# Batch 0 of a fused attention and FFN block: q turned elsewhere, weights in another order, and both ends of the kernel rearranged

## The chip, the core and the metric

The kernel runs on one core of a Trainium2 chip. The time is device microseconds of one execution, from launch to the last result; lower is better. Everything is float32.

The core's engines work in parallel, each through its own queue of instructions in order, and wait for each other by semaphores: TensorE (PE) for matmuls, VectorE (DVE), ScalarE (ACT), GpSimd (POOL), and SyncE (SP), which here only issues DMAs. ACT issues a few DMAs too.

## The reference

```python
x = L0_attn_x                                   # 8 x 1024 x 256
xn = layernorm(x)                               # no scale, no shift
q, k, v = split(xn @ qkv_w + qkv_b)             # 16 heads of 16
q, k = q / |q|, k / |k|                         # per head
kv  = einsum('bhnd,bhne->bhde', k, v)           # no softmax: 16 x 16 per head
att = einsum('bhnd,bhde->bhne', q, kv) @ proj_w + proj_b
ffn = relu(xn @ W1 + b1) @ W2 + b2              # 256 -> 1024 -> 256
out = x + att + ffn
```

## The kernel before

The kernel loops over the 8 batches. A batch is 1024 rows, 8 tiles of 128 rows (NT = 8, a half is HT = 4 tiles). The order of the work is written by hand: `tc.manual_schedule()` keeps each engine's instructions in the order in which the Python code issues them.

**Matmuls by sums.** Most products are done as 2 x 2 blocks with seven products instead of eight. That needs sums and differences of blocks of both operands: of W1 (`sums_of_w1`), W2 (`sums_of_w2`), the q,k weights (`sums_of_wqk`), the turned x (`sums_of_x`, `s3_of_x`), the hidden layer (`sums_of_h`), the turned q (`sums_of_q`) and k with x (`g_sums`). Nearly all of them run on POOL, through `sums_of_b` (L184-189) and `sums_of_a` (L191-197), four instructions each.

**A batch in steps.**
1. *Norm.* `norm_stats` (L254, L257, root on ACT L259), `norm_scale` (reciprocal L266, and `nmr` = -mean/std, L269), `norm_apply` on ACT (L278) or DVE (L282). For batch b+2 this is done during batch b.
2. *Turn of x.* `turn_x` transposes squares of 32 x 32 on DVE (L304) and lets 16 DMAs of SP (L306) bring each to its partitions. Batch 0 has no time for that: its tiles are transposed on PE and copied by ACT (`turn_tile`, L923, L924).
3. *`hidden(b)`*: twelve steps of `first`, `fifth` and `last` make the relu layer (L660 on PE, L672 on DVE, L667 on ACT). Between the steps, a table (`first_steps` for batch 0, `later_steps` otherwise) puts the small work: k^T x (`mix_g`), kv (`mix_kv`), kv @ proj_w (`mix_m`), scaling q by its norm (L488), turning q.
4. *`project_by_sums(b+1)`*: q and k of the next batch (L420 on PE, adds L426 on DVE, then on POOL the rest of the bias, L464, and k's scaling, L488). Batch 0 has its own `project` (L337, L343), which runs in the first 25 us and goes tile by tile.
5. *`second(b)`*: hidden @ W2 and q @ M in one accumulation (L785). In its middle, `mix_g_by_sums(b+1)` (L590) multiplies the sums that POOL has made of k and x (L557). Results are joined (L826), turned back on DVE (L817), added to x on POOL (L822) and stored by SP (L831).

**q in batch 0.** In every later batch q is turned by `turn_q`: four transposes on DVE and 16 DMAs of SP. Batch 0 uses `turn_on_pe` (L286-296): 16 transposes on PE (L292) into four banks of PSUM and four copies on ACT, between `hidden(0)` and `project_by_sums(1)`.

**The end.** In batch 7 the second half of the rows is turned back on PE (L838) and stored by ACT (L889) in three pieces, tiles 0 and 1, tile 2, tile 3. The first half goes the usual way: L817 on DVE, L822 on POOL, four stores of SP (L831).

**Buffers.** All bank-sized results share seven banks of PSUM. `turn_x`, `turn_q` and `g_sums` share one buffer ("turn"); q and k of all batches share one ("qk").

Of the kernel before, what the change touches and what calls it, by code (L numbers as in the profile page):

```python
# [9 lines left out]
F32 = mybir.dt.float32  # L10
AF = mybir.ActivationFunctionType
ALU = mybir.AluOpType
# [4 lines left out]
def kernel(  # L17
# [35 lines left out]
    P = 128  # L53
# [94 lines left out]

    def load_rest():

        load_halves(projw_sb, proj_w)
        load_halves(w2_sb, w2)
        for i, v in enumerate((proj_b, b2)):
            for j in range(R):
                nc.sync.dma_start(
                    out=ob[ts(j, S), i, :],
                    in_=v.rearrange("(j m c) -> j c m", m=2, c=S)[j],
                )
# [50 lines left out]
    def sums_of_w2():  # L209
        sums_of_b(  # L210
            nc.gpsimd, [w2_sb[:, ts(k, FH), ts(m, HC)] for k in range(2) for m in range(2)],
            [w2t[:, i, :, :] for i in range(3)],
        )
        nc.gpsimd.tensor_tensor(ob[:, 2, :], ob[:, 0, :], ob[:, 1, :], ALU.add)

    def halves(tt):
# [66 lines left out]
                    xn, xt, mv[:, i, 0:1], rstd[:, i : i + 1], ALU.subtract, ALU.mult  # L283
                )

    def turn_on_pe(dst, src, name, halves=(0, 1), copies=(nc.scalar.copy, nc.scalar.copy)):  # L286

        for h in halves:
            for kc in range(KC):
                tp = bank([P, HT, P], f"tp{name}_{h}_{kc}")  # L290
                for i in range(HT):
                    nc.tensor.transpose(tp[:, i, :], src[:, h * HT + i, ts(kc, P)], ident)  # L292
                copies[kc](
                    dst[:, kc, ts(h, HP), :, :].rearrange("p u m w -> p u w m"),
                    tp.rearrange("p (u w) m -> p u w m", w=2),
                )

    def turn(dst, src, name):


# [19 lines left out]
    def project(b, within={}, behind={}, held_to=0):  # L320

        xnT = xnTs[b]
        if b not in qks:
            qks[b] = one.tile([P, NT, 2 * C], F32, tag="qk", name=f"qk_{b}")
        qk = qks[b]
        late, held = [], []
        for h in range(2):
            ss = small.tile([P, HT, 2 * H], F32, tag="ssk" if h else "ssq", name=f"ss_{b}_{h}", bufs=1)  # L330
            for s in range(2):
                norms_of[b, h, s] = ss[:, :, ts(s, H)]
            for i in range(HT):
                t = h * HT + i
                pq = bank([P, 512], f"pq_{b}_{t}")
                for kc in range(KC):
                    nc.tensor.matmul(  # L337
                        pq, xnT[:, kc, t // 2, :, t % 2], wqkv_sb[:, kc, 0 : 2 * C],
                        start=(kc == 0), stop=(kc == KC - 1), skip_group_check=True,
                    )  # L340
                    if kc == 0:
                        within.get(t, lambda: None)()
                nc.vector.tensor_tensor(qk[:, t, :], pq, qkvb_sb[:, 0 : 2 * C], ALU.add)  # L343

                def square(t=t, ss=ss, i=i):
                    sq = work.tile([P, 2 * C], F32, tag="yt", name=f"sq_{b}_{t}")
                    nc.scalar.activation(sq, qk[:, t, :], AF.Square)
                    return lambda: nc.vector.tensor_reduce(
                        ss[:, i, :], sq.rearrange("p (g d) -> p g d", d=D), AX.X, ALU.add
                    )  # L350

                held.append(square)
                while held and t >= held_to:
                    late.append(held.pop(0)())
                    while len(late) > 1:
                        late.pop(0)()
                behind.get(t, lambda: None)()
        while late:
            late.pop(0)()
# [41 lines left out]
            sq.rearrange("p w (g d) -> p w g d", d=D), AX.X, ALU.add,  # L401
        )

    def project_by_sums(b):


        xnT, xS = xnTs[b], xSs[b]
        qks[b] = one.tile([P, NT, 2 * C], F32, tag="qk", name=f"qk_{b}")
        ss = small.tile([P, NT, H], F32, tag="ssk", name=f"ssk_{b}", bufs=1)
        a11, a12, s3, a22 = halves(xnT)  # L410
        s1, s2, s4 = xS
# [25 lines left out]
        for g in range(2):  # L437
            a, c_, d, e = (banks[g][s] for s in "acde")
            mm(a, a11, b11, g, True, False)
            u1 = add(tmp("u1", g), a, bk)  # L440
            mm(e, s1, t1, g, True, False)
            mm(c_, s2, t2, g, True, True)
            u2 = add(tmp("u2", g), c_, u1)
            u2s.append(u2)
            mm(d, s3, t3, g, True, False)
            u3 = add(tmp("u3", g), d, u2)
            add(part_of_qk(b, 1, g, 1), e, u3)
            while late:
                late.pop(0)()
            late.append(squares_of(b, 1, g, 1, ss))  # L450
# [34 lines left out]
    def scale(eng, b, h, s):  # L485
# [3 lines left out]
            part, part,  # L489
            norms_of[b, h, s].unsqueeze(3).to_broadcast([P, HT, H, D]), ALU.mult,  # L490
        )

    def scale_q(b, h):
        scale(nc.vector, b, h, 0)

    def turn_q(b):

# [242 lines left out]
    def first_steps(b):  # L740

        lo, hi, fold = range(HT), range(HT, NT), fold_bias_of_v()
        of_k, of_q = norms_of_first(1), norms_of_first(0)
        return {
            0: [lambda: load_squares(b), lambda: norm_apply(b + 1, lo)],
            1: [lambda: next(of_k)] * 3 + [lambda h=h: scale(nc.gpsimd, b, h, 1) for h in range(2)],
            2: [lambda: shift(b)],
            4: [
                lambda: norm_stats(b + 1, hi), lambda: norm_scale(b + 1, hi, True),
                lambda: norm_apply(b + 1, hi), lambda: next(of_q), lambda: next(of_q),  # L750
                lambda: next(of_q), lambda: mix_g(b), lambda: next(fold),
            ] + [lambda: turn_x(b + 1)] * R,
            5: [sums_of_w2, lambda: next(fold), lambda: next(fold)],
            6: [lambda: shift(b + 1), lambda: scale_q(b, 0)],
            7: [lambda: mix_kv(b)],
            8: [lambda: g_sums(b + 1, 0), lambda: scale_q(b, 1)],
            10: [lambda: mix_m(b)],
            11: [lambda: load(b + 2)],
        }

    def later_steps(b):
        return {
            0: [lambda: g_sums(b + 1, 0)] if b + 1 < B else [],
            1: [lambda: mix_kv(b)],
            2: [lambda: scale_q(b, 0)],
            3: [lambda: scale_q(b, 1)],
            4: [lambda: mix_m(b)],
            5: [lambda: turn_q(b)],
            6: [lambda: turn_q(b)],
            7: [lambda: turn_q(b)],  # L770
            8: [lambda: turn_q(b)],

            11: [lambda: sums_of_q(b)],
        }
# [15 lines left out]
    def second(b, early=lambda: None, between=lambda: None):  # L790
# [21 lines left out]
        def turn_back(n, m, y):  # L812

            yt = tmp("yt").rearrange("p a b c -> p (a b c)").rearrange(
                "p (u w r c) -> p u w r c", w=2, r=R, c=S
            )
            nc.vector.transpose(  # L817
                yt.rearrange("p u w r c -> p u r w c"),
                y.rearrange("p u (s r) w -> p u r w s", r=R),
            )  # L820
            xh = xq[:, n, :, :, ts(m, S)].rearrange("p r t c -> p t r c")
            nc.gpsimd.tensor_tensor(xh, xh, yt.rearrange("p u w r c -> p (u w) r c"), ALU.add)  # L822

        def join(n, m, bank_, u):
            y = tmp("y")
# [2 lines left out]

        def store(n):
            for j in range(R):  # L830
                nc.sync.dma_start(out=squares_v(out, b, n, j), in_=xq[ts(j, S), n])  # L831

        def back_on_pe(m, y, tiles, name):

# [94 lines left out]


    norm_stats(0, (0,))
    scale_and_apply(0)
    turn_tile(0)
    keep_warm(3)
    norm_stats(0, (1,))
    norm_stats(0, (2,))
    scale_and_apply(1)
    norm_stats(0, (3,))
    scale_and_apply(2)
    scale_and_apply(3)  # L940
# [3 lines left out]
    def tiles_2_3():  # L944
        for t in (2, 3):
            turn_tile(t)
        norm_stats(0, (4, 5))
        norm_stats(0, (6, 7))
        norm_scale(0, (4, 5), True)
        norm_scale(0, (6, 7), True)  # L950
        norm_apply(0, (4, 5))
        norm_apply(0, (6, 7))

    def tiles_4_to_7():
        for t in range(HT, NT):
# [13 lines left out]
        3,  # L969
    )  # L970
    norm_scale(1, range(HT), True)
    s3_of_x(0)
    sums_of_wqk()
    load_rest()
    for b in range(B):
        if b > 0:
            load_squares(b, (0,) if b == B - 1 else (0, 1))
# [3 lines left out]
                load(B, (HT, NT))  # L981
        hidden(b)
        if b == 0:
            qTs[0] = one.tile([P, KC, NP, P, 2], F32, tag="qT", name="qT_0")
            turn_on_pe(qTs[0], qks[0], "q_0")
            sums_of_q(0)
        if b + 1 < B:
            project_by_sums(b + 1)
            g_sums(b + 1, 1)

            def early():
                if b + 2 < B:
                    norm_stats(b + 2, range(NT))
                    norm_scale(b + 2, range(NT), True)

            def between():
                g_sums(b + 1, 2)
                norms_of_q(b + 1)

            out_parts = second(b, early, between)  # L1000
        else:
            out_parts = second(b)
# [41 lines left out]
```

## Time and profile before

| | us |
|---|---|
| median of 3 runs | 616.42 (616.12 to 616.46) |
| the profiled execution | 616.35 |
| its span, first to last instruction | 614.6 |
| PE busy in the span | 607.1 |
| DVE, POOL, ACT busy | 417.1, 421.4, 212.6 |
| PE's first matmul of the projection | 5.91 |
| last row of PE ends | 609.4 |
| last instruction of DVE ends | 609.7 |

The profile's times count from the first instruction of the span; some 1.8 us of the execution lie outside of it. In a row of a timeline the columns are start, duration, engine, line, operation, output and inputs, shape, and how many instructions were merged; a bracket names idle time of that engine before the row, and what ended it. A float32 matmul shows as two passes: 0.43 for 512 columns; a transpose of 128 x 128 takes 0.11.

### The profile page before, as it was taken

The numbers are of one execution on the slowest core, as the hardware profiler recorded it, in microseconds if no ns is written. First come the engines' busy times: TensorE is split into PE (matmuls) and PEld (weight loads), VectorE is DVE, ScalarE is ACT, GpSimd is POOL, SyncE is SP. The second block draws the span as 40 slices with busy tenths as digits, with TensorE's granted clock in tenths as the row PEclk, the third lists the DMA queues.
The fourth block names the chain that finished last, engine by engine and source line by source line (L and its number), as shares of the span: only waits on it lengthen the run. The fifth ranks groups of instructions, "written<-read, shape, count | busy, mean of one in ns | idle before, by whom it ended". The sixth has DMA issues, their size and how long they took to land.

```text
span 614.6 us, 6728 instructions
## 1 busy us (share of the span) xinstructions
PE 607.1 (99%) x2055; PEld 350.8 (57%) x2055; DVE 417.1 (68%) x746; ACT 212.6 (35%) x369; POOL 421.4 (69%) x345
## 2 busy tenths in 40 slices
PE   8999999999999999999999999999999999999996
PEld 5466765466644756447464484644755456644454
DVE  7886774876758776587665876577864777537823
ACT  4656223351324414243251532425223352103400
POOL 3699992699727995479944899349992499914701
PEclk9999999999999999999999999999999999999999
DMA  8633002760038400482005900158002550005302
GB/s 276 120 70 110 0 0 61 149 135 0 1 81 188 74 1 1 110 189 45 0 13 125 184 22 1 28 124 170 22 0 48 127 102 0 0 11 128 70 0 68
DMA packets 139940, 43.84 MB, mean 71 GB/s; under 512 B 135928, under 2 KB 136832, under 8 KB 139904
## 3 DMA queue, kind: packets, MB, share of 16 engines
q1 hardware_dynamic: 139184, 42.37, 31.1%
q10 hardware_dynamic: 720, 1.05, 0.5%
q8 instruction: 16, 0.26, 0.2%
q14 instruction: 20, 0.16, 0.1%
HBM read 20.32 MB, written 8.39 MB: 47 GB/s over the span
## 4 chain that ended last, share of the span: by engine, by line
PE 97%; DVE 1%; DMA 1%; ACT 0%; SPq 0%; issue 0%
PE poa L785 11%; PE poe L785 11%; PE pod L785 10%; PE pha L660 9%; PE phd L660 9%; PE phe L660 9%; PE poc L785 6%; PE phc L660 4%; PE pqa L420 4%; PE pqe L420 4%; PE pqd L420 4%; PE gpd L590 2%; PE gpe L590 2%; PE gpa L590 2%; PE pqc L420 2%; PE pq L337 1%
## 5 line engine op out<-in xcount | busy, mean ns | idle before, releaser
L822 POOL TENSOR_TENSOR xq<-xq,yt_o 128x512 f32<-128x512 f32 x30 | 38.0, 1265 | 127.3 <-DVE yt_o L817 127.3
L667 ACT ACTIVATE hT<-hT,b_sb 128x512 f32<-128x512 f32 x96 | 68.7, 721 | 61.4 <-DVE hT L672 56.7
L193 POOL TENSOR_TENSOR hS<-hT 128x512 f32<-128x512 f32 x31 | 47.0, 1517 | 34.3 <-ACT hT L667 34.3
L660 PE MATMUL pha<-xnT,w_sb 128*128 128x512 f32 x128 | 65.4, 592 | 0.0
L398 ACT ACTIVATE sq<-qk 128x512 f32<-128x512 f32 x56 | 33.8, 627 | 82.0 <-DVE qk L426 68.6
L785 PE MATMUL poa<-hT,w_sb 128*128 128x512 f32 x128 | 57.6, 592 | 0.0
L672 DVE TENSOR_TENSOR hT<-phe,u 128x512 f32<-128x512 f32 x64 | 43.7, 685 | 6.9 <-PE phe L660 5.3
L195 POOL TENSOR_TENSOR hS<-hT,hS 128x512 f32<-128x512 f32 x31 | 39.6, 1277 | 2.4
L817 DVE STREAM_TRANSPOSE yt_o<-y_o 128x512 f32<-128x512 f32 x30 | 33.3, 1109 | 11.7 <-ACT y_o L875 9.3
L194 POOL TENSOR_TENSOR hS<-hS,hT 128x512 f32<-128x512 f32 x31 | 39.5, 1273 | 2.4
L197 POOL TENSOR_TENSOR hT<-hT 128x512 f32<-128x512 f32 x31 | 41.0, 1322 | 0.0
L686 ACT COPY u<-pha 128x512 f32<-128x512 f32 x32 | 18.4, 575 | 56.8 <-PE pha L660 56.8
L785 PEld LDWEIGHTS poa<-hT,w_sb 128*128 128x128 f32 x128 | 23.8, 190 | 24.2 <-issue 23.9
L660 PEld LDWEIGHTS pha<-xnT,w_sb 128*128 128x128 f32 x128 | 23.7, 190 | 22.9 <-issue 22.2
L672 DVE TENSOR_TENSOR u<-phc,u 128x512 f32<-128x512 f32 x32 | 21.8, 680 | 19.6 <-ACT u L686 10.0
L667 ACT ACTIVATE hT<-pha,b_sb 128x512 f32<-128x512 f32 x32 | 21.8, 683 | 35.6 <-PE pha L660 35.6
L660 PE MATMUL phc<-xS,w1t 128*128 128x512 f32 x64 | 32.7, 592 | 0.0
L660 PE MATMUL phd<-xnT,w1t 128*128 128x512 f32 x64 | 32.7, 592 | 0.0
L660 PE MATMUL phe<-xS,w_sb 128*128 128x512 f32 x64 | 32.7, 592 | 0.0
L660 PE MATMUL phd<-xnT,w_sb 128*128 128x512 f32 x64 | 32.7, 592 | 0.0
L660 PE MATMUL phe<-xS,w1t 128*128 128x512 f32 x64 | 32.7, 592 | 0.0
L278 ACT ACTIVATE x<-x,nmr,rstd 128x256 f32<-128x256 f32 x60 | 30.6, 589 | 2.6 <-DVE nmr L269 2.6
(203 smaller groups left out, 1322.4 us busy)
## 6 DMA issues: line engine op xcount, KB each, us to landing
x<-in_L_attn_x_dram SPq DMA_DIRECT2D x15, 512.0 KB, 5.6
xq<-in_L_attn_x_dram SPq DMA_DIRECT2D x60, 128.0 KB, 3.5
out_dram<-xq SPq DMA_DIRECT2D x60, 128.0 KB, 2.9
xnT<-turn_x SPq DMA_DIRECT2D x112, 64.0 KB, 2.1
qT<-turn_q SPq DMA_DIRECT2D x112, 64.0 KB, 2.3
w_sb<-in_L_ffn_W_dram SPq DMA_DIRECT2D x2, 512.0 KB, 6.2
w_sb<-in_L_ffn_W_dram SPq DMA_DIRECT2D x8, 128.0 KB, 3.1
x<-in_L_attn_x_dram SPq DMA_DIRECT2D x3, 256.0 KB, 6.1
```

The lines of the kernel that those rows point to most:

```text
L193: eng.tensor_tensor(s1, a21, a22, ALU.add)
L194: eng.tensor_tensor(s2, s1, a11, ALU.subtract)
L195: eng.tensor_tensor(s4, a12, s2, ALU.subtract)
L197: eng.tensor_tensor(a21, a11, a21, ALU.subtract)
L398: nc.scalar.activation(sq, part_of_qk(b, n, g, m), AF.Square)
L420: nc.tensor.matmul(dst[:, w, :], a[:, g, :, w], rhs, start=start and w == 0, stop=stop, skip_group_check=True,)
L590: nc.tensor.matmul(dst, l[:, t, :], r[:, t, :], start=start and t == 0, stop=stop and t == HT - 1, skip_group_check=True,)
L660: nc.tensor.matmul(dst, lhsT, rhs, start=start, stop=stop, skip_group_check=True)
L667: nc.scalar.activation(block(i, n, m), src, AF.Relu, bias=b1_sb[:, fc : fc + 1])
L672: nc.vector.tensor_tensor(dst, p, q, ALU.add)
L785: nc.tensor.matmul(dst, l, r, start=start and n == 0, stop=stop and n == len(lhs) - 1, skip_group_check=True,)
L822: nc.gpsimd.tensor_tensor(xh, xh, yt.rearrange("p u w r c -> p (u w) r c"), ALU.add)
```

## The change

- **q of batch 0** is turned by `turn_q`, as in the other batches: its four DVE transposes and DMAs are two in steps 10 and 11 of `hidden(0)`, and two inside `project_by_sums(1)`, which takes steps to be run between its first products. Its scaling by the norm moves from DVE (steps 6 and 8) to POOL (step 5). `turn_on_pe` is gone.
- **W2 is loaded ahead of proj_w**, and `load_rest` is called ahead of `s3_of_x(0)`. `sums_of_w2` now runs there, and `sums_of_wqk` in step 5 of `hidden(0)`, where `sums_of_w2` was.
- **First tile by channel halves**: tile 0 is normed, transposed and copied in two halves of 128 channels, with tile 1's statistics between. Statistics of tiles 2 and 3 now follow the apply of tile 1. The pairs of tiles 4,5 and 6,7 are normed one after the other. The first add of `project` (tile 0) waits until tile 1's turn.
- **End**: in batch 7 the last add of half 0 runs on DVE, and two of half 0's four stores are issued by ACT.

On DVE the order of batch 0 becomes: M's copy, first turn of q, two adds of the hidden layer, second turn, the projection's first add, third turn, two adds, fourth turn, and then the first add that writes into the buffer that q and k share. On SP the 16 DMAs of q's turn are eight ahead of, and eight behind, the two loads of x of batch 2.

```diff
     def load_rest():
+        load_halves(w2_sb, w2)
         load_halves(projw_sb, proj_w)
-        load_halves(w2_sb, w2)
...
             [w2t[:, i, :, :] for i in range(3)],
         )
+
+    def sum_of_biases():
         nc.gpsimd.tensor_tensor(ob[:, 2, :], ob[:, 0, :], ob[:, 1, :], ALU.add)
...
-        late, held = [], []
+        late, held, adds = [], [], []
...
-                nc.vector.tensor_tensor(qk[:, t, :], pq, qkvb_sb[:, 0 : 2 * C], ALU.add)
+                adds.append(
+                    lambda t=t, pq=pq: nc.vector.tensor_tensor(
+                        qk[:, t, :], pq, qkvb_sb[:, 0 : 2 * C], ALU.add
+                    )
+                )
+                while adds and t > 0:
+                    adds.pop(0)()
...
-    def project_by_sums(b):
+    def project_by_sums(b, within=()):
...
             u1 = add(tmp("u1", g), a, bk)
+            for step in within[:1] if g == 0 else ():
+                step()
...
             u3 = add(tmp("u3", g), d, u2)
+            if g == 0:
+                for step in within[1:]:
+                    step()
+                qks[b] = one.tile([P, NT, 2 * C], F32, tag="qk", name=f"qk_{b}")
             add(part_of_qk(b, 1, g, 1), e, u3)
...
-            5: [sums_of_w2, lambda: next(fold), lambda: next(fold)],
-            6: [lambda: shift(b + 1), lambda: scale_q(b, 0)],
+            5: [lambda: next(fold), lambda: next(fold), sums_of_wqk, sum_of_biases]
+            + [lambda h=h: scale(nc.gpsimd, b, h, 0) for h in range(2)],
+            6: [lambda: shift(b + 1)],
             7: [lambda: mix_kv(b)],
-            8: [lambda: g_sums(b + 1, 0), lambda: scale_q(b, 1)],
-            10: [lambda: mix_m(b)],
-            11: [lambda: load(b + 2)],
+            8: [lambda: g_sums(b + 1, 0)],
+            10: [lambda: mix_m(b), lambda: turn_q(b)],
+            11: [lambda: turn_q(b), lambda: load(b + 2)],
...
-            nc.gpsimd.tensor_tensor(xh, xh, yt.rearrange("p u w r c -> p (u w) r c"), ALU.add)
+            eng = nc.vector if b == B - 1 and m == 1 else nc.gpsimd
+            eng.tensor_tensor(xh, xh, yt.rearrange("p u w r c -> p (u w) r c"), ALU.add)
...
-                nc.sync.dma_start(out=squares_v(out, b, n, j), in_=xq[ts(j, S), n])
+                queue = nc.scalar if b == B - 1 and j % 2 else nc.sync
+                queue.dma_start(out=squares_v(out, b, n, j), in_=xq[ts(j, S), n])
...
     norm_stats(0, (0,))
-    scale_and_apply(0)
-    turn_tile(0)
-    keep_warm(3)
-    norm_stats(0, (1,))
+    norm_scale(0, (0,), False)
+    i, mv, rstd = stats.pop((0, 0))
+    for kc in range(KC):
+        part = xs[0][:, 0, ts(kc, P)]
+        nc.vector.tensor_scalar(part, part, mv[:, i, 0:1], rstd[:, i : i + 1], ALU.subtract, ALU.mult)
+    norm_stats_1 = norm_stats_steps(0, (1,))
+    for kc in range(KC):
+        tp = bank([P, P], f"tpx_0_{kc}")
+        nc.tensor.transpose(tp, xns[0][:, 0, ts(kc, P)], ident)
+        nc.scalar.copy(xnTs[0][:, kc, 0, :, 0], tp)
+
+        for _ in norm_stats_1:
+            pass
+    keep_warm(2)
+
+    scale_and_apply(1)
     norm_stats(0, (2,))
-    scale_and_apply(1)
     norm_stats(0, (3,))
     scale_and_apply(2)
     scale_and_apply(3)
...
-        norm_stats(0, (4, 5))
-        norm_stats(0, (6, 7))
-        norm_scale(0, (4, 5), True)
-        norm_scale(0, (6, 7), True)
-        norm_apply(0, (4, 5))
-        norm_apply(0, (6, 7))
+        for pair in ((4, 5), (6, 7)):
+            norm_stats(0, pair)
+            norm_scale(0, pair, True)
+            norm_apply(0, pair)
...
+    load_rest()
     s3_of_x(0)
-    sums_of_wqk()
-    load_rest()
+    sums_of_w2()
...
         if b == 0:
-            qTs[0] = one.tile([P, KC, NP, P, 2], F32, tag="qT", name="qT_0")
-            turn_on_pe(qTs[0], qks[0], "q_0")
-            sums_of_q(0)
+
+            def last_turn():
+                turn_q(0)
+                sums_of_q(0)
+
+            project_by_sums(1, [lambda: turn_q(0), last_turn])
+        elif b + 1 < B:
+            project_by_sums(b + 1)
```

More of the change, by code (lines that the diff above doesn't have):

```diff
@@ L284, in norm_apply @@
                 )
[L286 to L296, printed above, removed]
     def turn(dst, src, name):
@@ L402, in squares_of @@
         )
-    def project_by_sums(b):
+    def project_by_sums(b, within=()):
         xnT, xS = xnTs[b], xSs[b]
-        qks[b] = one.tile([P, NT, 2 * C], F32, tag="qk", name=f"qk_{b}")
         ss = small.tile([P, NT, H], F32, tag="ssk", name=f"ssk_{b}", bufs=1)
@@ L491, in scale @@
         )
-    def scale_q(b, h):
-        scale(nc.vector, b, h, 0)
     def turn_q(b):
@@ L764, in later_steps @@
             1: [lambda: mix_kv(b)],
-            2: [lambda: scale_q(b, 0)],
-            3: [lambda: scale_q(b, 1)],
+            2: [lambda: scale(nc.vector, b, 0, 0)],
+            3: [lambda: scale(nc.vector, b, 1, 0)],
             4: [lambda: mix_m(b)],
@@ L983 @@
         if b == 0:
-            qTs[0] = one.tile([P, KC, NP, P, 2], F32, tag="qT", name="qT_0")
-            turn_on_pe(qTs[0], qks[0], "q_0")
-            sums_of_q(0)
+            def last_turn():
[4 more added lines that the diff above has]
+            project_by_sums(b + 1)
         if b + 1 < B:
-            project_by_sums(b + 1)
             g_sums(b + 1, 1)
```

## The prediction

> **What bounds the kernel now.** I read the page first, then the chain that ended last, then the timelines of the stretches that the diff touches.
>
> ```profile
> PE 607.1 (99%) x2055; PEld 350.8 (57%) x2055; DVE 417.1 (68%) x746; ACT 212.6 (35%) x369; POOL 421.4 (69%) x345
> ...
> PEclk9999999999999999999999999999999999999999
> ```
>
> TensorE (PE) is busy 607.1 of 614.6 us at full clock. So a gain has three possible places: work taken off PE, the first 15 us, and the 5 us after PE's last matmul. The chain (start, duration, work) shows the start and the one piece of PE work that the change removes:
>
> ```profile
> 10.92 1.07 DVE nmr L269
> ...
> 12.10 1.27 DVE nmr L269
> ...
> 13.40 1.10 ACT x L278 x2
> ...
> 15.13 7.93 PE pq L337 x18
> ...
> 56.39 1.75 PE tpq L292 x16
> ```
>
> From 15.1 on PE never pauses for long, but before that it follows VectorE's norms. The 16 transposes of q cost 1.75. The timelines of DVE and POOL between 10 and 14 us tell why two instructions on 2 columns take over 1 us:
>
> ```profile
> 10.76 0.13 DVE L266 RECIPROCAL rstd<-rstd 128x2 f32<-128x2 f32 x1
> 10.92 1.07 DVE L269 SCALAR_TENSOR_TENSOR nmr<-mv,rstd 128x2 f32<-128x2 f32 x1
> ...
> 12.10 1.26 DVE L269 SCALAR_TENSOR_TENSOR nmr<-mv,rstd 128x2 f32<-128x2 f32 x1
> ...
> 10.71 1.26 POOL L189 TENSOR_TENSOR w1t<-w_sb 128x512 f32<-128x512 f32 x1 [9.40 <-DMA w_sb<-in_L_ffn_W_dram]
> 12.07 1.27 POOL L189 TENSOR_TENSOR w1t<-w_sb,w1t 128x512 f32<-128x512 f32 x1
> 13.30 1.27 POOL L189 TENSOR_TENSOR w_sb<-w_sb 128x512 f32<-128x512 f32 x1
> ```
>
> Each nmr ends when the POOL instruction that began before it ends (11.99 and 11.97; 13.36 and 13.34). The nmr at 25.94 does so too (26.44, POOL's piece of wqk ended at 26.43). An nmr thus waits for a whole POOL instruction if it comes second. Last, POOL is nearly PE's equal in batch 0:
>
> ```profile
> 89.12 1.28 POOL L557 TENSOR_TENSOR gt<-qk,gs 128x512 f32<-128x512 f32 x1
> 90.36 1.29 POOL L557 TENSOR_TENSOR gs<-x,gs 128x512 f32<-128x512 f32 x1
> ...
> 90.80 1.06 PE L590 MATMUL gpa<-qk,x 128*128 128x128 f32 x8
> 91.81 1.13 PE L590 MATMUL gpd<-gt,x 128*128 128x128 f32 x8
> ```
>
> The groups of L590 follow each other at 0.89, so gpd was due at 91.69 and started at 91.81, after POOL's last sum ended at 91.65. POOL runs without a pause from 46.30 to there. PE can become earlier here only by what POOL becomes earlier.
>
> **The change, part by part.** Times are those of the profiled execution: span 614.6, 616.35 in all. The median of the runs is 616.42, 0.07 above.
>
> *Start.* Half an apply of tile 0 costs about 0.26 (between the 0.41 of 256 columns and the 0.18 of 64), so tile 0's first half is on PE 0.15 earlier and the first pq matmul 0.3. That is lost again: the statistics of tile 1 come 0.02 later, those of tile 3 now follow tile 1's apply (aggregate at 7.40 for 7.31), and ACT copies tile 1 behind tile 3's root, about 0.1 later. Value: nothing, PE some 0.1 late up to 13.1. Then the pairs 4,5 and 6,7. Tile 4,5's root stands on ACT behind the copies of tiles 2 and 3 (10.08 before, 10.17 now), reciprocal 10.51 to 10.67, nmr at 10.70. POOL's first sum of W1 starts at 10.71. This is a tie, and it decides the start. *Nmr first:* 0.15 for it, ACT applies tiles 4,5 from 10.9, the root of 6,7 follows at 11.9, reciprocal 12.2, nmr 12.4, which waits for POOL's second sum, 13.36 as before. The add of q,k of tile 0 is now behind it on DVE (ends 13.96), and tile 4's transposes need that bank; PE resumes at 15.1 to 15.2 for 15.06: +0.1. *POOL first:* nmr ends 11.98, ACT's applies 12.0 to 13.1, root 13.3, reciprocal 13.5; that nmr now meets POOL's third sum (13.30 to 14.57): 14.59 for 13.36. +1.2.
>
> *W2 first, sums of W2 and wqk exchanged.* W2's eight DMAs are issued from 10.3 (before: 17.2 to 22.7) behind x of batch 1, and were landed 2 to 3 us after their issue; POOL wants W2 at 23.5. Projw comes to W2's old time and is wanted at 52.8. Cost nothing; without that cover POOL would wait for W2's last landing, 25.4 before. On POOL four sums of W2 (5.03) take the place of five of wqk (3.59), inside a wait that lasted until 30.28. The nmr of 25.94 now meets W2's second sum, which ends at about 26.15: 0.25 earlier, and with it k's scaling. This is worth it: PE's gp matmuls, due at 32.34, had waited 0.16 for k's second half.
>
> *q's scale to POOL, and POOL's account.* From 39.23 POOL did W2 (5.03), the bias (0.66), waited 1.38, and its next four sums ran 6.95, drawn out by VectorE's two scales (2.03 and 2.27 instead of 1.27): at 53.20 it was free. Now: wqk 3.59, bias 0.15, two scales 3.83, half a us that it waits for VectorE's L514, four sums 5.2: 52.5. With the 0.25, POOL is 0.95 earlier than before relative to the start.
>
> *q turned by DVE and DMAs.* PE loses 16 x 0.11 = 1.75, ACT four copies (2.16), DVE two scales (1.21 and 1.65) and gains four transposes (2.43 for four, L304). The first stands after M's copy (54.5), the others between adds of the projection: the adds behind them have idle time before them (1.93, 1.03, 0.17); I find the pqe add 0.5 late, caught up two adds later, no bank late. The first turn waits until the DMAs of turn_x have read its buffer (landed by 53); were these late, the hidden adds behind it would stall PE. DMAs: 16 more on SP, at 0.65 each, with the two loads of x (1.01) between them: issued 54.6 to 66.5, last landing near 69. PE wants q's turn at 71.8, POOL at 72.3. Nothing, with 3 us of cover.
>
> Here a rule speaks against the change. The Trainium skill, DMA: Bandwidth & Descriptors, Rules for kernel authors, wants many small transfers joined, since under 64 KB overhead is most of the cost, and its section on the anatomy of one DMA (written for those that GpSimd issues) has a fixed part of about 2.0 us. If each of the 16 paid that one after another, q would land at 54.6 + 32 = 87, and PE would stall 15 us. The trace's row: 16 of 64 KB for x in 10.53 us, landing 2.1 after issue; the fixed part overlaps. I take the row.
>
> *So the middle:* PE could be 1.75 + 0.16 earlier, POOL 0.95. With the start's 0.1, POOL's last sum ends at 91.65 - 0.95 + 0.1 = 90.8 and gpd starts at 90.9 instead of 91.81: -0.9 (nmr first); with the start's 1.2, +0.2 (POOL first). Later batches keep their order.
>
> *End.* The last add of half 0 takes about 0.68 on DVE (L197 of the same size there) instead of 1.27 on POOL, so the stores start at 606.2 for 606.81. It stands before the add of L843 and pod's join: that moves from 606.09 to 606.62, PE's last transposes by 0.15 to 0.25. SP took 3.33 to issue four stores; now two queues take two each, done by 607.5, in time for ACT's own at 608. The last landings were 613.69 (SP) and 613.59 (ACT). The Trainium skill, same page, Issuing engines are not separate DMA queues, says that all DMAs run on the same 16 engines, so that a second queue saves issue time only: then the end moves by the earlier start, -0.6. By the rows, ACT's last store, issued at 610.0, lands 2.6 (SP's first store) to 3.2 later (ACT's second): -0.5 to -1.1. I take -0.8; bounds +0.2 (contention as before, PE later) and -1.3.
>
> Sum, nmr first: -0.9 - 0.8 = -1.7, so 614.65, at the median 614.7; POOL first: +0.2 - 0.8 = -0.6, at the median 615.8. What no row shows: what a turn in the projection does to banks (0 to +0.6), and what the early W2 does to loads in flight (+-0.3).
>
> **Rivals.** *A, nmr before POOL, 614.7:* chance 0.50; its own range 613.8 to 615.4. *B, POOL before nmr, 615.8:* the start's 1.2 eats the middle. For it: arrival and start are 0.01 apart. Against: nothing but that tie. 0.28. *C, the later nmr (25.94) misses W2's second sum* and waits for the third: 1.2 later, POOL's account lost, 615.9 after A, 617.0 after B. The margin is 0.15 us, so 0.12. *D, slower: q's turn lands late.* POOL's sums of q are in front of the scaling of k and the sums that PE waits for at gpd, so every us by which the last of the DMAs lands after 72.3 is a us for PE. For it: two loads of 512 KB, 4.6 us to landing, stand in the midst of them. It would have to land after 72.3 + 1.7 = 74.0 to cancel A's gain, and after 75.3 to be seen as slower; at 76.5 the time is 614.7 + 4.2 = 618.9. Against: that is 5 to 7 us later than the rows give. 0.10. *That the transposes leave nothing* (POOL's bound holds all of it) is part of B.
>
> **How the numbers follow.** A measurement of this kernel can tell about 0.2% (1.23 us) from no change: faster is under 615.2, slower above 617.65. A gives 0.47 of faster and 0.03 of same; B 0.06 and 0.22; C 0.01 and 0.11; D 0.01 of same and 0.09 of slower. Together 0.54, 0.37, 0.09. The range goes from A's low bound with a better end (613.5) to B with an end that brings little (616.4); about 0.05 lies below, 0.13 above.
>
> **What would show it.** A: nmr of tiles 4,5 takes about 0.15 and PE's unbroken run starts near 15.2; B: it takes over 1 us and PE starts near 16.3. The nmr near 26 ends with a POOL sum of W2. No tpq rows. PE waits at gpd for POOL's gs by about 1 us, at 90.9. The last qT landing is before 71. The stores of half 0 start near 606.2 relative to a PE end as before, on two queues. I am wrong if PE has a new wait between 54 and 72, or if the end after PE's last matmul is not shorter.

## The result and the profile after

| | before | changed |
|---|---|---|
| median of 14 runs each, us | 616.43 | 615.73 |
| profiled execution, us (span) | 616.35 (614.6) | 615.58 (613.8) |

The ratio of the changed kernel to the one before is 0.9994, 95% interval 0.9985 to 1.0002: 0.7 us by the medians, and the interval takes in 1, that is, no change. The forecast had 614.7 as the likeliest time and 615.8 for its case B; the trace shows case B. Medians are compared here and below because in 17 of the 100 executions of the changed kernel, E2, E4, E5 and E7 to E9, the variants with the new start and its nmr on VectorE, the time lies 1.5 to 2.6 us above the variant's median, at a mean granted TensorE clock of 0.995 to 0.997.

The page of the changed kernel, its first lines:

```profile
span 613.8 us, 6725 instructions
...
PE 606.2 (99%) x2038; PEld 349.6 (57%) x2038; DVE 418.3 (68%) x750; ACT 210.7 (34%) x366; POOL 422.0 (69%) x346
```

PE lost 0.9 us of busy time and the span lost 0.8. The chain of what ended last (start, duration, work), its beginning:

```profile
8.48 1.13 PE pq L327 x2
...
10.95 0.89 DVE nmr L271
...
11.86 0.90 ACT x L280 x2
...
13.37 1.04 DVE nmr L271
...
14.43 1.10 ACT x L280 x2
...
16.17 7.93 PE pq L327 x18
```

PE's unbroken run is in the chain from 16.17, where before it was from 15.13: the start is a full microsecond worse. Both nmr stood in the chain before too, but one behind the other on VectorE; now ACT's application of tiles 4 and 5 and the root of tiles 6 and 7 lie between them. VectorE's (DVE) and POOL's timelines between 10 and 15 us (start, duration; in brackets the idle time before and what ended it), with two lines of PE's:

```profile
10.75 0.17 DVE L268 RECIPROCAL rstd<-rstd 128x2 f32<-128x2 f32 x1 [1.03 <-ACT rstd L261]
10.95 0.87 DVE L271 SCALAR_TENSOR_TENSOR nmr<-mv,rstd 128x2 f32<-128x2 f32 x1
...
13.37 1.03 DVE L271 SCALAR_TENSOR_TENSOR nmr<-mv,rstd 128x2 f32<-128x2 f32 x1
...
10.54 1.26 POOL L189 TENSOR_TENSOR w1t<-w_sb 128x512 f32<-128x512 f32 x1 [9.24 <-DMA w_sb<-in_L_ffn_W_dram]
...
13.11 1.27 POOL L189 TENSOR_TENSOR w_sb<-w_sb 128x512 f32<-128x512 f32 x1
...
15.09 0.93 PE L926 MATMUL tpx<-ident,x 128*128 128x128 f32 x4 [1.16 <-ACT x L280]
```

The first nmr came at 10.95, 0.41 behind POOL's first sum of W1 (10.54), and ended with it (11.82 and 11.80); the second came at 13.37, behind the third sum (13.11), and ended with that (14.40 and 14.38). Tile 4 and 5's transposes were done by 13.93; those of tiles 6 and 7 then waited 1.16 for x.

The turn of q by DMAs, as the trace tells of qT and of the chain near it:

```profile
L296 SPq DMA_DIRECT2D qT<-turn_q x16: 585/610/1642, 56.0 to 68.4; - x16
...
DMA to landing us min/median/max: 2.1/2.3/6.6
...
69.32 4.29 PE poa L785 x10
```

PE ran through poa, whose last two products read qT from 72.6, without a pause. Between 54 and 72 us it waited for nothing. It came to the first gpa, the first mixing product of batch 1, at 86.32 instead of 87.23, 0.91 earlier, and lost most of that within the mixing products. VectorE, POOL and PE there (PEld is PE's load of weights):

```profile
82.47 1.59 DVE L271 SCALAR_TENSOR_TENSOR nmr<-mv,rstd 128x8 f32<-128x8 f32 x1
83.98 0.68 DVE L809 TENSOR_TENSOR u_o<-pod,u_o 128x512 f32<-128x512 f32 x1
...
89.06 0.65 DVE L827 SCALAR_TENSOR_TENSOR y_o<-poe,ob,u_o 128x512 f32<-128x512 f32 x1
89.75 1.12 DVE L817 STREAM_TRANSPOSE yt_o<-y_o 128x512 f32<-128x512 f32 x1
...
91.14 0.29 DVE L595 TENSOR_TENSOR u_g<-gpd,u_g 128x128 f32<-128x128 f32 x1
...
80.21 3.83 POOL L490 TENSOR_TENSOR qk<-qk,ssk 128x1024 f32<-128x1024 f32 x2
...
90.14 1.29 POOL L556 TENSOR_TENSOR gs<-x,gs 128x512 f32<-128x512 f32 x1
...
90.12 1.16 PE L589 MATMUL gpa<-qk,x 128*128 128x128 f32 x8
91.58 1.13 PE L589 MATMUL gpd<-gt,x 128*128 128x128 f32 x8 [0.30 <-DVE u_g L595]
...
91.55 0.97 PEld L589 LDWEIGHTS gpd<-gt,x 128*128 128x128 f32 x8 [0.46 <-POOL gs L556]
```

The second gpd starts at 91.58, 0.23 earlier than before (91.81); the group ahead of it had started at 90.12, so at the pace of 0.89 it was due near 91.0. The profile names two causes: for the products VectorE's u_g, for the load of their weights POOL's last sum, gs. Both ended at 91.43, and the second is what the prediction had taken for the cause. The names speak against it: this gpd reads gt, which POOL had finished at 90.19, and gs is read by the gpe behind it; u_g in turn reads the bank that this gpd adds to, so gpd has to wait until it is done. The chain that ended last goes through VectorE's nmr here, where before it had been PE throughout:

```profile
82.47 1.59 DVE nmr L271
...
88.19 0.95 DVE ssq L363
...
91.58 1.13 PE gpd L589 x8
```

The experiment E5 tells the two apart.

The end, on VectorE and on the two queues:

```profile
603.23 0.75 DVE L827 SCALAR_TENSOR_TENSOR y_o<-poe,ob,u_o 128x512 f32<-128x512 f32 x1 [2.40 <-PE poe L785]
...
605.23 0.69 DVE L823 TENSOR_TENSOR xq<-xq,yt_o 128x512 f32<-128x512 f32 x1
...
605.98 1.26 SPq L834 DMA_DIRECT2D out_dram<-xq  x2
...
605.99 1.60 ACTq L834 DMA_DIRECT2D out_dram<-xq  x2
607.97 2.85 ACTq L892 DMA_DIRECT2D out_dram<-x  x3
```

The stores start 0.83 earlier than before (606.81). From the start of this y_o to the end of the span it is 10.6 us; before, it was 11.1 (603.46 to 614.6).

### The profile page after: what moved, and what is told of

Read it like the earlier page. It is cut to its first block, busy times and chain, and to the rows that moved or that the text cites. A ratio compares the mean times of both kernels' runs of the same rounds, so it can differ in the third digit from the quotient of the medians.

```text
span 613.8 us, 6725 instructions
## 1 busy us (share of the span) xinstructions
PE 606.2 (99%) x2038; PEld 349.6 (57%) x2038; DVE 418.3 (68%) x750; ACT 210.7 (34%) x366; POOL 422.0 (69%) x346
## 4 chain that ended last, share of the span: by engine, by line
PE 95%; DVE 3%; ACT 1%; DMA 0%; issue 0%; DVEq 0%; ACTq 0%
PE poa L785 11%; PE poe L785 10%; PE pod L785 10%; PE pha L659 9%; PE phe L659 9%; PE phd L659 9%; PE poc L785 6%; PE phc L659 4%; PE pqa L416 4%; PE pqd L416 4%; PE pqe L416 4%; PE pqc L416 2%; PE gpd L589 2%; PE gpe L589 2%; PE gpa L589 2%; PE pq L327 1%
## 5 line engine op out<-in xcount | busy, mean ns | idle before, releaser
L823 POOL TENSOR_TENSOR xq<-xq,yt_o 128x512 f32<-128x512 f32 x29 | 36.7, 1264 | 125.0 <-DVE yt_o L817 125.0
```

The source lines that it names most:

```text
L823: eng.tensor_tensor(xh, xh, yt.rearrange("p u w r c -> p (u w) r c"), ALU.add)
```

## The experiments

Each median is of 5 to 21 runs. E1 to E4 ran on one chip, E5 to E8 on another and E9 to E12 on a third, each group beside runs of the kernel before on its chip; the last column is the difference of the two medians.

| | median us | before us | ratio (95%) | difference |
|---|---|---|---|---|
| E1 old start | 614.89 | 616.38 | 0.9977 (0.9970 to 0.9985) | -1.49 |
| E2 new start only | 617.47 | 616.38 | 1.0021 (1.0013 to 1.0029) | +1.09 |
| E3 new end only | 615.67 | 616.38 | 0.9990 (0.9982 to 0.9999) | -0.71 |
| E4 turn on PE | 616.87 | 616.38 | 1.0014 (1.0005 to 1.0023) | +0.49 |
| E5 later nmr moved | 615.00 | 616.34 | 0.9985 (0.9979 to 0.9992) | -1.34 |
| E6 first nmr on ACT | 614.49 | 616.34 | 0.9976 (0.9969 to 0.9983) | -1.85 |
| E7 one queue | 615.73 | 616.34 | 0.9999 (0.9989 to 1.0008) | -0.61 |
| E8 last add on POOL | 616.42 | 616.34 | 1.0009 (1.0001 to 1.0017) | +0.08 |
| E9 q scaled by VectorE | 616.50 | 616.27 | 1.0006 (0.9997 to 1.0014) | +0.23 |
| E10 = E1 + E5 | 614.24 | 616.27 | 0.9966 (0.9953 to 0.9978) | -2.03 |
| E11 = E6 + E5 | 613.68 | 616.27 | 0.9960 (0.9946 to 0.9973) | -2.59 |
| E12 = E11, turn on PE | 615.33 | 616.27 | 0.9985 (0.9979 to 0.9992) | -0.94 |

Against the changed kernel (-0.70) an experiment's effect is its difference plus 0.70.

**E1 and E2: the start.** E1 is the changed kernel with the start of before; E2 is before with the new start.

```diff
-    norm_scale(0, (0,), False)
-    i, mv, rstd = stats.pop((0, 0))
-    for kc in range(KC):
-        part = xs[0][:, 0, ts(kc, P)]
...
+    scale_and_apply(0)
+    turn_tile(0)
+    keep_warm(3)
+    norm_stats(0, (1,))
...
-        for pair in ((4, 5), (6, 7)):
-            norm_stats(0, pair)
-            norm_scale(0, pair, True)
-            norm_apply(0, pair)
+        norm_stats(0, (4, 5))
+        norm_stats(0, (6, 7))
+        norm_scale(0, (4, 5), True)
+        norm_scale(0, (6, 7), True)
+        norm_apply(0, (4, 5))
+        norm_apply(0, (6, 7))
```

> The changed kernel with the first tiles as before: tile 0 normalized whole and turned through one bank, three warming transposes, statistics, scales and applications of tiles 4 to 7 in before's order, and each bias add of the projection straight behind its products. The rest is as changed. Theory (the new start loses about 1 us, because nmr of tiles 4 and 5 waits out a sum of W1 on POOL, and POOL's chain shifts with the start as PE does): PE's unbroken run begins at about 15.1 us instead of 16.1, gpd's second half starts about 1.0 earlier than in the changed kernel, and the time is 614.7 (-1.0 against the changed kernel, -1.7 against before). Rival (PE's start is slack, since POOL's chain sets gpd and does not move with it): 615.7, as the changed kernel.

> Before with nothing but the new start: tile 0 by channel halves, two warming transposes, pairs of tiles one after the other, the bias adds of the projection held back by a tile. Theory: nmr of tiles 4 and 5 meets POOL's first sum of W1, x of tile 5 lands about 1 us later, PE's run begins near 16.1, and all that follows shifts: 617.4 (+1.0). Rival (the new start is neutral or good by itself, and the late second was from something else in the changed kernel): 616.2 to 616.5.

E1 gave 614.89, 0.79 better than the changed kernel; E2 617.47, 1.09 worse than before. In E1's chain:

```profile
12.11 1.27 DVE nmr L271
...
13.41 1.10 ACT x L280 x2
...
15.15 7.93 PE pq L327 x18
```

PE's run is back at 15.15. In E2 the first nmr took 1.18 (10.87 to 12.05) and the second 1.03, and PE's run begins at 16.40. So the new start by itself costs +1.09, where the forecast of case B had +1.2. E2's times range from 616.66 to 619.02. In its profiled execution, of 619.02, PE's granted clock was 0.59 from 17.0 to 21.2 us, so of that trace only the first 17 us are read.

**E6: is it the wait of nmr?** In E6 nmr of batch 0's two pairs is made by ACT, from mv in its place; the rest is the changed kernel, new start included.

```diff
+            if b == 0:
+                nmr = mv[:, :, 0]
+                nc.scalar.mul(nmr, nmr, -1.0)
+                for k in range(len(tiles)):
+                    nc.scalar.mul(nmr[:, k : k + 1], nmr[:, k : k + 1], rstd[:, k : k + 1])
...
             nc.vector.scalar_tensor_tensor(nmr, mv[:, :, 0], -1.0, rstd, ALU.mult, ALU.mult)
```

> The changed kernel, in which nmr of batch 0's pairs and of nothing else is made by ACT (one negation beside the reciprocal, one multiplication for each tile) instead of VectorE's scalar_tensor_tensor. Theory (VectorE's nmr waits out POOL's sums of W1[...], 0.87 and 1.03 us where 0.2 would do, and this costs the start its second; ACT's instructions do not meet it): x of tiles 4 and 5 starts near 11.4 instead of 11.86, x of tiles 6 and 7 near 13.3 instead of 14.43, PE's stall of 1.3 us at 15.1 falls to 0.3 or less, 614.7 (-1.0 against the changed kernel). Rival (ACT's six more instructions cost as much as they save, or the stall comes from something else in the new order): 615.5 to 615.8.

614.49: 1.15 better than the changed kernel, and better than with the old start. ACT's timeline and the chain:

```profile
10.92 0.48 ACT L274 ACTIVATE mv<-mv,rstd 128x1 f32<-128x1 f32 x2 [0.21 <-DVE rstd L268]
11.30 1.08 ACT L286 ACTIVATE x<-x,mv,rstd 128x256 f32<-128x256 f32 x2
...
12.86 0.48 ACT L274 ACTIVATE mv<-mv,rstd 128x1 f32<-128x1 f32 x2 [0.20 <-DVE rstd L268]
...
14.97 7.93 PE pq L333 x18
```

Two multiplications of 128x1 on ACT take 0.48 together (and a negation ahead of them 0.20, while VectorE makes the reciprocal) beside the same sums on POOL, where VectorE's nmr took 0.87 and 1.03. PE's run is in the chain from 14.97, earlier than before the change. So what the new start lost (1.09 in E2) it lost to nmr's wait. Whether its order is better than the old one is not shown: the old start with nmr on ACT was not run.

**E4: what the turn is worth.** The changed kernel with before's `turn_on_pe`:

```diff
-            10: [lambda: mix_m(b), lambda: turn_q(b)],
-            11: [lambda: turn_q(b), lambda: load(b + 2)],
+            10: [lambda: mix_m(b)],
+            11: [lambda: load(b + 2)],
...
-            project_by_sums(1, [lambda: turn_q(0), last_turn])
-        elif b + 1 < B:
+            turn_on_pe(qTs[0], qks[0], "q_0")
+            sums_of_q(0)
+        if b + 1 < B:
             project_by_sums(b + 1)
```

> The changed kernel with q of batch 0 turned by PE's 16 transposes and ACT's copies, as before, behind the hidden layer; q is still scaled on POOL in the fifth step and the projection follows the turn. Theory (POOL's chain through the sums for gpd binds PE there, and PE waited 0.8 us for it in the changed kernel): of the 1.75 us that PE spends again on the turn 0.8 is paid out of that wait: 616.7 (+1.0 against the changed kernel). Rival 1 (PE is the bound all the way): 617.5 (+1.75). Rival 2 (POOL is the bound all the way and does not feel the turn): 615.7, as the changed kernel.

616.87: the turn on PE costs 1.19 more, of the 1.75 us that PE spends on it. Most of the other 0.56 is what the changed kernel loses at gpd and E4 does not: from its first gpd to its second it took 2.56 (89.02 to 91.58), E4's later PE 2.11 (90.73 to 92.84).

**E5: who makes PE wait at gpd?** Reciprocal and nmr of batch 2 leave their place between the additions for poc and pod:

```diff
             def early():
                 if b + 2 < B:
                     norm_stats(b + 2, range(NT))
-                    norm_scale(b + 2, range(NT), True)
+                    if b > 0:
+                        norm_scale(b + 2, range(NT), True)
...
         if b + 2 < B:
+            if b == 0:
+                norm_scale(b + 2, range(NT), True)
             norm_apply(b + 2, range(NT))
```

> The changed kernel, in which reciprocal and nmr of batch 2 (128x8) are issued only behind the mixing sums of batch 1, instead of between the additions for poc and pod of batch 0. In the changed kernel's trace nmr took 1.60 us there (82.47 to 84.06) and ended with POOL's scaling of k (84.04); the addition for pod, the four ssq, their root and reciprocal, y_o, yt_o and u_g stood behind it on VectorE, and PE waited 0.11 for gpa's u_g and 0.47 for gpd's u_g. Theory 1 (that chain on VectorE, held by POOL[...], is what binds PE there, not the data of POOL's sums): the chain comes over 1 us earlier, PE does not wait at gpd, 615.1 (-0.6 against the changed kernel). Theory 2, as in the prediction (PE waits for POOL's own sums): POOL is not moved, 615.7, no change. Against theory 1: the moved nmr meets another POOL instruction and holds back x of batch 2 by 1.3 us, which PE does not need then.

615.00, 0.64 better than the changed kernel; POOL's own sums were not moved. VectorE's and PE's timelines:

```profile
82.23 0.69 DVE L809 TENSOR_TENSOR u_o<-pod,u_o 128x512 f32<-128x512 f32 x1 [0.37 <-PE pod L785]
...
90.26 0.29 DVE L595 TENSOR_TENSOR u_g<-gpd,u_g 128x128 f32<-128x128 f32 x1 [0.41 <-PE gpd L589]
...
93.37 0.17 DVE L271 SCALAR_TENSOR_TENSOR nmr<-mv,rstd 128x8 f32<-128x8 f32 x1
...
90.06 1.06 PE L589 MATMUL gpa<-qk,x 128*128 128x128 f32 x8
90.95 1.06 PE L589 MATMUL gpd<-gt,x 128*128 128x128 f32 x8
```

The addition for pod now starts at 82.23 instead of 83.98, u_g waits for PE and no longer PE for u_g, and gpd follows gpa at 0.89. The moved nmr took 0.17. POOL's last sum still ended at 91.46, half a us behind the start of gpd at 90.95, so gpd does not need it; gpe, which does, started at 91.84. So PE had waited for VectorE's chain, which nmr held up: in the changed kernel it came at 82.47 and ended with POOL's scaling of k (84.06 and 84.04).

**E9: or does POOL's load matter after all?** q of batch 0 is scaled by VectorE as before, which takes 4.27 us off POOL.

```diff
-            + [lambda h=h: scale(nc.gpsimd, b, h, 0) for h in range(2)],
-            6: [lambda: shift(b + 1)],
+            6: [lambda: shift(b + 1), lambda: scale(nc.vector, b, 0, 0)],
...
-            8: [lambda: g_sums(b + 1, 0)],
+            8: [lambda: g_sums(b + 1, 0), lambda: scale(nc.vector, b, 1, 0)],
```

> The changed kernel with q of batch 0 scaled by VectorE in the sixth and eighth step, as before, so that POOL's two scalings of 4.27 us together (43.62 to 47.89) are gone; the turn stays with VectorE and the DMAs. Theory (POOL reaches PE at gpd[...]: its scaling of k ends some 1.9 us earlier, since its sums of q can then begin when qT has landed, near 70.9 instead of 72.76, and nmr of batch 2 meets a shorter POOL instruction, ending near 83.4 instead of 84.06): PE's wait at gpd goes from 0.47 to about 0: 615.2 (-0.5). Rival 1 (VectorE is late by its 4.3 us, q's turn is issued later and qT lands after 71.8): PE stalls at poa, 616 or more. Rival 2: no change, 615.7.

616.50, 0.93 worse. The theory was wrong in its first link, and rival 1, right on the size, was wrong on the cause: the turn was issued when it had been. POOL, VectorE and PE:

```profile
46.88 2.15 POOL L193 TENSOR_TENSOR hS<-hT 128x512 f32<-128x512 f32 x1 [3.20 <-ACT hT L666]
...
51.70 2.26 POOL L197 TENSOR_TENSOR hT<-hT 128x512 f32<-128x512 f32 x1
...
46.69 1.22 DVE L490 TENSOR_TENSOR qk<-qk,ss 128x1024 f32<-128x1024 f32 x1
...
51.17 1.65 DVE L490 TENSOR_TENSOR qk<-qk,ss 128x1024 f32<-128x1024 f32 x1
...
59.19 1.14 PE L416 MATMUL pqc<-wt,xS 128*128 128x256 f32 x4 [0.22 <-POOL xS L231]
```

POOL, with less to do, was later: it stood still for 3.20 us until ACT had made hT, and then two of its sums took 2.15 and 2.26 instead of 1.27, for VectorE's scales had begun before them. 3.20 + 0.88 + 0.99 = 5.07 is more than the 4.27 saved. POOL left these sums at 53.96 (53.05 in the changed kernel), the sums of x of batch 1 were 0.9 late, and PE stalled for them at pqc and at pqd behind it, some 0.8 in all.

**E3, E7, E8: the end.** E3 is before with the new end only. E7 and E8 are the changed kernel with one half of the new end each:

```diff
-                queue = nc.scalar if b == B - 1 and j % 2 else nc.sync
-                queue.dma_start(out=squares_v(out, b, n, j), in_=xq[ts(j, S), n])
+                nc.sync.dma_start(out=squares_v(out, b, n, j), in_=xq[ts(j, S), n])
...
-            eng = nc.vector if b == B - 1 and m == 1 else nc.gpsimd
-            eng.tensor_tensor(xh, xh, yt.rearrange("p u w r c -> p (u w) r c"), ALU.add)
+            nc.gpsimd.tensor_tensor(xh, xh, yt.rearrange("p u w r c -> p (u w) r c"), ALU.add)
```

(the first edit alone is E7, the second alone E8)

> Before with nothing but the new end: the last addition of half 0 of the last square on VectorE instead of POOL, its four stores shared out over SP's and ACT's queues. Theory (the addition is done 0.6 earlier, the landings another little earlier by the second queue; PE's last products are delayed by at most 0.3 by the addition on VectorE): 615.7 (-0.7). Rival (the last stores of the other half, behind them in ACT's queue, take the place: the end is set by ACT's last store, which waits for ACT's two more issues): 616.3 to 616.5.

> The changed kernel with all four stores of the last square's half 0 from SP's queue, the last addition still on VectorE. Theory (what the end gains is the earlier start of these stores, done 0.9 us earlier by VectorE; a second queue saves only issue time, four issues of about 0.65 each from 606.0 end at 608.6 and land ahead of the others): 615.8 (+0.1 against the changed kernel). Rival (the second queue is what brought the landings forward): 616.2 or more, most of the 0.7 lost again.

> The changed kernel with the last addition of half 0 on POOL as before, its four stores still from two queues. Theory (the start of the stores counts): they are issued 0.9 us later (606.85), ACT's two issues reach to 608.3 and hold back its first store of the other half by 0.3, while PE's last turns come 0.3 earlier without VectorE's addition: 616.0 to 616.4, most of the 0.7 lost. Rival (the second queue counts): 615.7.

E3 gave 0.71 less than before. E7 lost 0.09 of it, E8 all (0.78). The same is seen in the profiled runs, as the time from the start of the last y_o to the end of the span: before 11.1, E8 11.2 (603.10 to 614.3), changed 10.6, E3 10.6 (603.35 to 613.9), E7 10.5 (603.41 to 613.9). E7's queue of SP:

```profile
606.16 2.63 SPq L832 DMA_DIRECT2D out_dram<-xq  x4
```

Four issues in 2.63 are done at 608.8, ahead of the last two stores of the other half. The gain comes with the addition on VectorE; the second queue brings nothing that these runs can tell.

**E10, E11, E12: together.** E10 joins E1 and E5, E11 joins E6 and E5, and E12 is E11 with q turned by PE.

> Two of the pieces together: the changed kernel with the first tiles as before, and with nmr of batch 2 behind the mixing sums. Theory (two different losses, so they add): -0.8 and -0.7 as measured alone: 614.2. Rival (PE, earlier by the first, meets POOL's own sums for gpd, so that the second brings little): 614.8.

> The two repairs of the changed kernel together: nmr of batch 0's pairs on ACT, nmr of batch 2 behind the mixing sums. Theory (they add, -1.2 and -0.7 as measured alone; PE then runs from the start to the end without a stall of over 0.2): 613.8. Rival (POOL's last sums for gpd, which end at 90.24 with the first repair, come too late for an earlier PE, whose gpe would begin near 90.7): 614.4.

> As the kernel with both repairs, but with q of batch 0 turned by PE's transposes, as before. Theory (with the waits on VectorE gone PE is the bound, and the turn costs it its full 1.75): 615.55, or 1.75 more than the kernel with both repairs. Rival (a bound beside PE still takes part of it, as in the changed kernel, where the turn on PE cost 1.1): 1.1 more or less.

The pieces add: against the changed kernel E10 brings 1.33 (0.79 + 0.64 = 1.43), E11 1.89 (1.15 + 0.64 = 1.79). E11 at 613.68 is the shortest of all, 2.59 below the kernel before and 1.89 below the changed one. Its PE goes through the mixing products of batch 1 at an even 0.89:

```profile
89.06 1.06 PE L595 MATMUL gpa<-qk,x 128*128 128x128 f32 x8
89.96 1.06 PE L595 MATMUL gpd<-gt,x 128*128 128x128 f32 x8
90.85 1.06 PE L595 MATMUL gpe<-qk,gs 128*128 128x128 f32 x8
```

With these two waits gone the turn is worth 1.65 (E12 less E11), nearly PE's 1.75.

## Why the prediction was right and wrong

- **Start: the choice that failed.** The prediction saw the collision and priced it well (+1.2; E2 +1.09, and 0.79 back in E1), but gave it 0.28 against 0.50, on a lead of 0.01 us between two worked-out times. It gave 0.54 to a time under 615.2, which did not come; that the time lies in its range is owed to case B. nmr was to be at 10.70 and POOL's sum at 10.71; they were at 10.95 and 10.54. The step at fault is a term of the sum: "ACT copies tile 1 behind tile 3's root, about 0.1 later". The copy came 0.34 later (first before the change, then changed):

```profile
7.72 0.37 ACT L924 COPY xnT<-tpx 128x256 f32<-128x256 f32 x1
...
8.06 0.37 ACT L927 COPY xnT<-tpx 128x256 f32<-128x256 f32 x1
```

Tile 3's aggregate, forecast for 7.40, began at 7.64, so its root on ACT began at 7.86 (before 7.52); 0.09 of it is that the first x landed later in this execution. PE waited 0.38 for the copy, its transposes of tiles 2 and 3 and ACT's copies of them were 0.33 late (9.87 for 9.54), the root behind these copies began at 10.41 instead of 10.17, and the reciprocal at 10.75 instead of 10.51. That alone put nmr behind POOL's sum; W1's landing, which started POOL 0.17 earlier, widened the gap. It was no coin that fell the wrong way: in the profiled executions of all seven kernels with this start (the changed one, E2, E4, E5, E7 to E9) nmr began at 10.86 to 10.97 and POOL's sum at 10.41 to 10.77, nmr behind it each time. Of the 1.03 us between 614.7 and 615.73, the old start gives 0.79 back (E1).
- **W2 first, and the nmr near 26: right.** In the changed kernel that nmr started at 26.98 and took 0.22, ending with W2's second sum, as worked out, and gp's products ran without a gap (7.07 for 7.26 before). Case C did not come.
- **q's turn: right, and less roomy than said.** There are no rows of tpq, and PE did not wait. The last issue was at 68.4, where 66.5 had been worked out, one landing took 6.6 us (the first issued behind the two loads of x), and the last four, issued up to 68.4, took 2.4 to 4.7. POOL took its first sum of q at 72.8 and did not wait for them. The first eight, issued at 0.65 each, landed 2.1 to 2.2 after their issue: what the prediction read from x's row, that these times overlap, holds for q.
- **The bound at gpd: right in size, wrong in its cause.** "PE can become earlier here only by what POOL becomes earlier" took two ends that coincide for one cause. Before the change POOL's last sum ended at 91.65 and VectorE's u_g at 91.67:

```profile
91.38 0.29 DVE L596 TENSOR_TENSOR u_g<-gpd,u_g 128x128 f32<-128x128 f32 x1
```

The lines that the prediction shows already tell that the last sum writes gs, and that gpd reads gt, which ended at 90.40. E5 gets the time back without touching POOL's work. POOL did rule the time of u_g, but through nmr, which waits out POOL's scaling of k; so the gain at gpd followed POOL's clock, and the sum came near. E9 does not test this, for there POOL became later. For case B +0.2 was forecast at gpd and -0.23 measured: the start cost 1.04 instead of 1.2 (16.17 for 15.13), and POOL won about 1.2 instead of 0.95 relative to it. POOL's data is the next bound and near: in E11 its last sum ends at 90.47, and gpe starts at 90.85.
- **End: right in size, by the wrong one of two reasons.** -0.8 was taken, -0.71 measured (E3), within the rows' -0.5 to -1.1. The rule of the Trainium skill that was set against it (DMA: Bandwidth & Descriptors, Issuing engines are not separate DMA queues) said -0.6, all from the earlier start. E7 (0.09 lost) and E8 (0.78 lost) side with the rule: the earlier start is all that can be seen, and the added 0.2 for the second queue had no ground.
- **The sum of case B**: 615.8 forecast, 615.73 measured. That they agree within 0.1 is in part luck. In the two profiled executions gpd is 0.43 earlier than forecast, and from the last y_o to the end of the span 0.6 is gained (11.14 to 10.57) instead of 0.8. The single experiments give +1.09 (E2) or +0.79 (E1) for the start, -0.71 (E3) for the end and -1.19 (E4) for the turn, which leaves +0.11 to +0.41 for the rest (order of W2 and wqk, q's scale on POOL) and for what the parts do to each other; no run takes that apart.

That an nmr which begins second ends only with POOL's instruction is seen at 10.95, 13.37 and 82.47, and that POOL waits so for VectorE in E9. The Trainium skill, SBUF — State Buffer, Who interferes with whom, states it: an instruction of VectorE with two inputs in SBUF shares a port with POOL's reads, and whoever issues first keeps it for its whole instruction. The trace agrees also where it says who is spared: nmr has mv and rstd in SBUF and waits; additions with one input in PSUM (in E5 0.69 for u_o, from 82.23, within POOL's scaling of k of 80.26 to 84.09) and the statistics of tiles 6 and 7 (in E6 0.73 for two, 10.73 to 11.46, within POOL's first sum of 10.64 to 11.92) do not.

## What to carry to other kernels

When a small instruction lies at a wait's end, ask what it shares with which engine, not what it costs alone: an instruction on 8 columns, 0.17 us alone, took 1.59 here, and moving two such steps, one to ACT (1.15) and one behind the critical chain (0.64), gave 1.89 together, where the whole change gave 0.70. Two ends that lie within 0.03 us of each other cannot be told apart by their times: read on which of the two the waiting work depends, by its inputs and by the buffer it writes, then move one. A tie in a forecast is a sign that its terms have to be worked out finer, or that the collision should be taken out of the kernel; here the side that lost had a term 0.2 too small.

## What was not expected of the hardware

Work taken off a busy engine can make it later: POOL without its 4.27 us of scaling was 0.9 later, because the pause it got was spent on waiting for ACT, and VectorE's 128x1024 scales, once begun, held two of its sums by 0.88 and 0.99 us (E9). VectorE's addition ahead of PE's last turns made the last addition of x 0.28 later after y_o than with the add on POOL (6.25 against 5.97 us from y_o's start, changed kernel and E8), yet the end came earlier. And PE's granted clock fell to 0.59 from 17.0 to 21.2 us in E2's profiled execution, after PE had waited 1.47 us up to 15.32. In the changed kernel's profiled execution PE waited 1.16 there and kept its full clock, so what lowers it stays open.
